# Last MLP's norm between other products, a second PSUM bank, and a later preparation, in a four-layer network

## Chip, cores and metric

The kernel runs on one core of a Trainium2 chip. The metric is the time of one execution on the device in microseconds (us); lower is better.

## What is computed

The network takes x of shape (8, 384, 32, 32), all in float32, through four layers. Two are Mamba-like (a layer norm, a projection, a short causal convolution, a selective scan over 1024 tokens with 16 states per channel, an output projection); the second of them has a gate from an attention pool, and an MLP after it. Two are depthwise convolutions with 13x13 support, the last with a pointwise product in front and a GELU behind. The change touches the MLP at the end of the second layer and the preparation of the convolutions' tables:

```python
        xs = xs + mo
        h = _ln(xs, n3_g, n3_b)
        h = jax.nn.gelu(h @ fc1_w.T + fc1_b) @ fc2_w.T + fc2_b
        xs = xs + h
...
    def bn_eval(y, gamma, beta, mean, var):
        inv = gamma * lax.rsqrt(var + BN_EPS)
        return y * inv[None, :, None, None] + (beta - mean * inv)[None, :, None, None]
```

## The kernel before

**Tiling.** An image has 1024 tokens, handled as two halves of 512. Channels lie on partitions: 384 channels are 3 tiles of 128 (KC), the inner 768 are 6 (KD), the MLP's 1536 are 12 (KF). The two Mamba layers are done as 32 units, each one image half of one layer; a unit is 48 slots of the scan. The scan itself keeps VectorE (the recurrence, L553 and L556, and the products with C, L561), ScalarE (the decays, L525) and GpSimd (the inflows, L532) busy.

**The order.** All else is placed by hand: `put(slot, f, ...)` puts a piece of work into a slot (with `first=True` ahead of the others of that slot), and the loop at L911 emits the pieces slot by slot; after the last scan step `plan.rest()` (L929) emits what is left. Within one engine, and within SP's queue, the instructions run in exactly that order, so a waiting instruction holds everything behind it on its engine. The slots stand in the table `AT` (L220) relative to a unit or an MLP. The unit's own loops end at slot 1536; slots after that are the tail.

**An MLP half.** `Mlp(b, half)` (L688) is image b, half 0 or 1; I write (7,0) and (7,1) for the last two. Its norm (`norm`, L726, slots `mlp_norm`) loads `mx` (L367), takes the mean with a product (L372), subtracts it on VectorE (L375), squares on ScalarE (L379), sums by product (L385), takes ln and exp on ScalarE (L390 to L394), and does a Newton step and the scaling on GpSimd (L400 to L409). Then come 12 "up" products of three matmuls (`mlp_up`, L695, each with a weight slice `wi` of 192 KB, five buffers), each copied out of PSUM by ScalarE (`mlp_raw`, L699), GELU in four batches of three (`table`, L456, with a table load ahead and another, L305, behind), and 3 "down" products of 12 matmuls (`mlp_down`, L708, each with two weight halves `wo` of 384 KB, three buffers). VectorE adds bias and residual (`mlp_out`, L714; the residual `mo` has one buffer) into `rows_out`, one buffer, which SP stores into `x3` (`mlp_store`, L721). Up and down products share one PSUM bank (`ps_f`, tag f); means, variances and the units' products use the two banks of `mm()` (L300).

**Around them.** The last unit's output projection (`out_product`, L604, `out_gate`, `out_add`, `out_store`, slots `out`) writes the half of `x2` that MLP (7,1) reads. `prepare` (L111) is a generator of 26 pieces, one slot each from `AT["prepare"]`: four small norms on ScalarE and VectorE, two bias vectors written to memory and read back over GpSimd's queue, six tables (load over GpSimd's queue, VectorE, store over GpSimd's queue), and at last `spread` (L148): two products and two ScalarE copies. The first unit's step sizes times u (`step_u`, L495) follow on GpSimd.

**After them.** `Depthwise` (L932) and `Pointwise` (L1006) lie in SBUF and PSUM partly where the layers' tiles were. A tile that reuses a place waits for the last use of the tile there. GpSimd fills their borders (L952) and loads the first ten groups of weights `wt` (L959, four DMAs of 128 KB each) and the images `xp` (L973).

Of the kernel before, what the change touches and what calls it, by code (L numbers as in the profile page):

```python
# [9 lines left out]
F32 = mybir.dt.float32  # L10
AF = mybir.ActivationFunctionType
ALU = mybir.AluOpType
# [4 lines left out]
P = 128  # L17
B = 8
C = 384
# [6 lines left out]
T = 512  # L26
NU = B * L // T
# [39 lines left out]
class Plan:  # L67
# [6 lines left out]
    def put(self, slot, f, *args, first=False):  # L74
        self.slots.setdefault(slot, ([], []))[0 if first else 1].append(lambda: f(*args))
# [141 lines left out]

AT = {'in_ahead': 3, 'out_ahead': 2, 'taps_ahead': 4, 'norm': (-5, -2, -1, 0, 1, 2, 3, 3, 4, 6, 8, 8, 12, 13, 14), 'x': (14, 16, 18, 24, 26, 29), 'shift': 1, 'conv': 4, 'u': 5, 'silu': ((28, 3, 0), (34, 6, 1), (40, 6, 3), (57, 6, 6)), 'hid': 2, 'ranks': (33, 34, 35), 'z': (31, 34, 36, 38, 40, 41), 'B': (40, 42, 47, 48), 'C': (42, 45, 48, 52), 'repeat': (9, 12, 12, 13), 'out': (0, 5, 9), 'out_half': 3, 'out_add': 4, 'out_gate': 2, 'res_ahead': 1, 'heads': 15, 'softmax': (16, 17, 18), 'attend': (19, 22, 25, 26), 'context': 27, 'hidden': (29, 30, 32, 35, 36, 39), 'gates': (47, 41, 46), 'mlp': 22, 'mlp_norm': (-7, 0, 1, 2, 3, 4, 5, 5, 5, 6, 6, 10, 10, 12, 12), 'mlp_plan': ((3, 62, 12, (21, 31, 42, 69), -2), (2, 42, 6, (24, 30, 42, 46), -2), (2, 40, 4, (24, 26, 34, 40), -2), (2, 42, 3, (24, 26, 34, 36), -2), (2, 42, 6, (24, 24, 36, 36), -2)), 'fold0': (-145, -128), 'shifted': 1, 'bc_out': 36, 'store': 2, 'px_ahead': 2, 'pool': (0, 4), 'norm0': (-97, -89, -86, -85, -83, -80, -77, -75, -74, -73, -72, -71, -69, -69, -68), 'soft': ((37, 2), (45, 4), (62, 6)), 'du': 1, 'du_pace': 0, 'flat_u': 1, 'inject': 0, 'y': 25, 'fold': 0, 'var': 1, 'down_gap': 0, 'first': {'x': (2, 4, 7, 10, 13, 16), 'silu': ((14, 3, 0), (22, 6, 0), (34, 6, 2), (44, 6, 6)), 'ranks': (23, 24, 26), 'z': (29, 29, 31, 33, 34, 35), 'soft': ((29, 2), (33, 4), (60, 6)), 'bc_out': 27, 'B': (32, 34, 36, 39), 'repeat': (0, 0, 1, 3), 'C': (38, 44, 44, 47)}, 'fold0_step': (1, 8), 'norm1': (-2, 0, 2, 2, 3, 4, 5, 5, 9, 9, 11, 11, 13, 14, 14), 'prepare': (-67, 4),  # L220
}


def layers(tc, k, a, vec, x0, x1, x2, x3, lasting, got):
# [8 lines left out]
    nc = tc.nc  # L233
# [7 lines left out]
    with ExitStack() as st:  # L241
# [5 lines left out]
        ps_f = st.enter_context(tc.tile_pool(name="m_f", bufs=1, space=PSUM))  # L247
# [8 lines left out]
        t = tile("fh")  # L256
# [25 lines left out]
        rows_out = wp.tile([P, T // HW, WIDE], F32, name="rows_out")  # L282
# [81 lines left out]

        def load(s, src, tag):
            s.xt = work.tile([P, KC, T], F32, tag=tag, name=tag, bufs=1)
            nc.sync.dma_start(s.xt, src.rearrange("(c p) t -> p c t", p=P)[:, :, s.cols])  # L367

        def mean(s):
            s.mean = mm()  # L370
# [25 lines left out]
        def rs_newton(s, step):  # L396

            if step == 0:
                s.rt = work.tile([P, T], F32, tag="sq", name="sq", bufs=1)
                nc.gpsimd.tensor_tensor(s.rt, s.ry, s.ry, ALU.mult)  # L400
            elif step == 1:
                nc.gpsimd.tensor_tensor(s.rt, s.rt, s.rv, ALU.mult)
            elif step == 2:
                nc.gpsimd.tensor_scalar(s.rt, s.rt, -0.5, 1.5, ALU.mult, ALU.add)
            else:
                nc.gpsimd.tensor_tensor(s.ry, s.ry, s.rt, ALU.mult)

        def scale(s, c):
            nc.gpsimd.tensor_tensor(s.xt[:, c], s.xt[:, c], s.ry, ALU.mult)  # L409


        def product(s, m):
# [274 lines left out]
        class Mlp:  # L687
            def __init__(self, b, half):  # L688
                self.b, self.half, self.cols = b, half, slice(half * T, (half + 1) * T)
                self.w, self.ps, self.hs = {}, {}, [None] * KF  # L690

        def mlp_up(s, m, c):
            if c == 0:
                s.ps[m] = ps_f.tile([P, T], F32, tag="f", name="f")
            nc.tensor.matmul(s.ps[m], s.w["in", m][:, c], s.xt[:, c], start=c == 0, stop=c == KC - 1)  # L695

        def mlp_raw(s, m):
# [6 lines left out]

        def mlp_down(s, m, f):
            if f == 0:
                s.down = ps_f.tile([P, T], F32, tag="f", name="f")
            nc.tensor.matmul(  # L708
                s.down, s.w["out", 2 * m + f // KD][:, f % KD], s.hs[f], start=f == 0, stop=f == KF - 1
            )  # L710
# [7 lines left out]

        def mlp_store(s, m):
            n = T // HW  # L720
            nc.sync.dma_start(x3[m * P : (m + 1) * P, s.half * n : (s.half + 1) * n, s.b, :], rows_out)  # L721
# [44 lines left out]
        for b in range(1, B):  # L766
            order += [(1, b - 1), (0, b + 1)] if b < B - 1 else [(1, b - 1), (1, b)]
        units = [Unit(both[n], b, half) for n, b in order for half in range(L // T)]
        done = {(s.layer.gated, s.b, s.half): i for i, s in enumerate(units)}
        assert len(units) == 2 * NU  # L770

        for i, s in enumerate(units):

            lay, at = s.layer, (i - 1) * SLOTS
            first = AT if i else {**AT, **AT["first"]}
            norm(s, lay.src[s.b], "xt", at, AT["norm"] if i > 1 else AT[f"norm{i}"])
            for d in range(KD):
                e = at + first["x"][d]
# [44 lines left out]
            for d in range(KD):  # L823
                at = i * SLOTS + (d - 2) * PER
# [48 lines left out]
        for b in range(B):  # L873
            for half in range(L // T):
                s = Mlp(b, half)
                at = max(at, (done[True, b, half] + 1) * SLOTS + AT["mlp"])
                if (at - AT["mlp"]) % SLOTS > 20:
                    at += (AT["mlp"] - at) % SLOTS
                pace_up, down, pace_down, tables, gap = AT["mlp_plan"][max(b - B + 4, 0) + (b == B - 1) * half]
                norm(s, x2[b], "mx", at, AT["mlp_norm"])  # L880
                for m in range(KF):
                    e = at + 12 + pace_up * m
                    use_in(e, s, m, fc1_w[m])
                    for c in range(KC):
                        put(e + c * pace_up // KC, mlp_up, s, m, c)
                    put(e + 2 * pace_up // KC + 1, mlp_raw, s, m, first=True)
                for j, e in enumerate(tables):
                    put(at + e, table, lambda s=s, j=j: s.hs[3 * j : 3 * j + 3], AF.Gelu_apprx_tanh)
                for m in range(KC):
                    e = at + down + (pace_down + AT["down_gap"]) * m  # L890
                    put(e, mlp_residual, s, m)
                    for f in range(KF):
                        if f % KD == 0:
                            use_out(e + f * pace_down // KF, s, 2 * m + f // KD, a["fc2"][2 * m + f // KD])
                        put(e + f * pace_down // KF, mlp_down, s, m, f)
                    put(e + pace_down, mlp_out, s, m, first=True)
                    put(e + pace_down + AT["store"], mlp_store, s, m, first=True)
                at += down + KC * (pace_down + AT["down_gap"]) + gap
# [316 lines left out]
```

## Time and profile before

| | |
|---|---|
| median of 3 runs | 6908.87 us (6908.8 to 6910.72) |
| the profiled execution's own time | 6907.97 us |
| its span, first to last instruction | 6906.2 us |
| mean granted TensorE clock | 0.923 |
| busy, PE / VectorE / ScalarE / GpSimd | 85% / 83% / 65% / 77% of the span |
| from 6200 to 6380 us: PE / VectorE / ScalarE / GpSimd busy | 144.76 / 9.07 / 52.43 / 48.80 us |
| from 6382 to 6555 us: PE busy, DMA share | 168.65 of 173 us, 1.04 |

The span falls into a start (to about 150 us), the scan loop (to about 6200), the tail of products (to 6380) and the convolutions (to the end). A line of a timeline gives start, duration, engine, line, operation, output <- inputs, shape, number of instructions, and in brackets the idle time ahead of it and what ended that. A line of the chain of waits gives start, duration, engine and line. "SPq" and "POOLq" are DMA issues on those engines' queues. Averages over the whole span say little about a single stretch: what counts is which wait ends last in it.

### The profile page before, as it was taken

The page shows a single profiled execution, that of the slowest core. Times are in us where ns is not written, and L with a number is a line of the kernel's source. Part 1 is how long each engine was busy: PE and PEld are TensorE (multiplying, and loading weights), DVE is VectorE, ACT ScalarE, POOL GpSimd, SP SyncE. Part 2 cuts the span into 40 slices and gives each one's busy share as a digit, 9 for nine tenths or more (in the row PEclk, how much of TensorE's full clock was granted, in tenths as well). Part 3 has the DMA queues.
Part 4 walks back from the last instruction along what each step waited for, and adds up shares of the span by engine and source line. Part 5 has one row for each costly group of instructions (what it writes and reads, how often), then busy time and mean ns, then how long its engine had stood idle before and what let it go on. Part 6 is the DMA issues. An engine that isn't in the chain of part 4 may idle for free. (4 is left out here: it accounts for less than half of the span.)

```text
span 6906.2 us, 76841 instructions
## 1 busy us (share of the span) xinstructions
PE 5876.6 (85%) x22562; PEld 2090.7 (30%) x22562; DVE 5750.3 (83%) x4591; ACT 4477.5 (65%) x7478; POOL 5295.9 (77%) x2864
## 2 busy tenths in 40 slices
PE   6877788888888888888888888889898888977988
PEld 2222222222322232222222232223232222323645
DVE  3899988999889888888888889888888898780837
ACT  4776666867676766767676767777677567652222
POOL 3888888888888878888888888887878888672412
PEclk7888888999999999999999999999999889989999
DMA  4665555666666666666666666666665665754979
GB/s 131 166 174 154 155 156 151 166 174 167 174 163 171 161 173 160 164 162 172 166 165 167 169 175 160 164 168 169 159 172 163 160 173 155 170 116 119 287 214 234
DMA packets 944770, 1160.04 MB, mean 168 GB/s; under 512 B 301264, under 2 KB 537344, under 8 KB 944352
## 3 DMA queue, kind: packets, MB, share of 16 engines
q1 hardware_dynamic: 788672, 1060.83, 58.7%
q10 hardware_dynamic: 140736, 50.09, 3.0%
q0 software_dynamic: 14944, 44.20, 2.3%
q8 instruction: 183, 3.00, 0.2%
q14 instruction: 235, 1.93, 0.1%
HBM read 904.67 MB, written 199.49 MB: 160 GB/s over the span
## 5 line engine op out<-in xcount | busy, mean ns | idle before, releaser
L532 POOL TENSOR_TENSOR dbu<-B,ru 128x1024 f32<-128x1024 f32 x1536 | 3585.9, 2360 | 163.0 <-DMA B<-bc 88.9
L525 ACT ACTIVATE h<-rd,A 128x512 f32<-128x512 f32 x3072 | 2117.2, 690 | 882.0 <-DVE hc L561 532.1
L553 DVE TENSOR_TENSOR_SCAN h<-h,state,dbu 128x512 f32<-128x512 f32 x1152 | 1482.6, 1287 | 208.2 <-ACT h L525 75.6
L561 DVE TENSOR_TENSOR hc<-h,C 128x1024 f32<-128x1024 f32 x1152 | 1411.1, 1225 | 146.1 <-DMA C<-bc 21.7
L556 DVE TENSOR_TENSOR_SCAN h<-h,dbu 128x1024 f32<-128x1024 f32 x576 | 1317.8, 2288 | 223.2 <-ACT h L525 156.7
L572 POOL TENSOR_TENSOR hc<-dbu,C 128x1024 f32<-128x1024 f32 x384 | 904.0, 2354 | 722.6 <-DVE dbu L556 388.0
L583 PE MATMUL acc<-hc,fold 128*32 128x512 f32 x6144 | 1151.2, 663 | 327.3 <-DVE hc L561 248.8
L415 PE MATMUL mm<-xt,wi 128*128 128x512 f32 x2232 | 1126.8, 643 | 58.4 <-ACT delta L491 19.4
L695 PE MATMUL f<-mx,wi 128*128 128x512 f32 x1152 | 606.5, 634 | 145.8 <-ACT fh L699 113.4
L415 PEld LDWEIGHTS mm<-xt,wi 128*128 128x128 f32 x2232 | 423.0, 202 | 763.4 <-issue 444.0
L604 PE MATMUL mm<-u,wo 128*128 128x512 f32 x1152 | 597.7, 660 | 65.6 <-DMA wo<-in_l_out_dram 65.4
L708 PE MATMUL f<-fh,wo 128*128 128x512 f32 x1152 | 582.6, 624 | 71.0 <-DMA wo<-in_fc_dram 60.1
L583 PEld LDWEIGHTS acc<-hc,fold 128*32 128x32 f32 x6144 | 162.5, 112 | 1131.1 <-DVE hc L561 517.4
L553 DVE TENSOR_TENSOR_SCAN dbu<-h,state,dbu 128x512 f32<-128x512 f32 x384 | 470.5, 1267 | 14.7 <-ACT h L525 8.4
L556 DVE TENSOR_TENSOR_SCAN dbu<-h,dbu 128x1024 f32<-128x1024 f32 x192 | 438.1, 2282 | 51.4 <-ACT h L525 50.6
L439 PE MATMUL mm<-xp,taps 128*64 128x512 f32 x1536 | 412.6, 658 | 21.1 <-ACT xp L425 8.1
L973 POOL DMA_DIRECT2D xp<-x x192 | 123.5, 644 | 386.7 <-PE ps L997 196.7
L997 PE MATMUL ps<-xp,wt 128*32 128x256 f32 x6144 | 345.7, 384 | 34.8 <-ACT o L1002 21.3
L305 ACT ACT_TABLE_LOAD x289 | 370.8, 1283 | 5.8 <-PEq L1203 0.7
L604 PEld LDWEIGHTS mm<-u,wo 128*128 128x128 f32 x1152 | 233.1, 211 | 435.6 <-issue 366.8
L695 PEld LDWEIGHTS f<-mx,wi 128*128 128x128 f32 x1152 | 209.9, 196 | 502.1 <-issue 252.8
L425 ACT ACTIVATE xp<-mm,b_in 64x512 f32<-64x512 f32 x384 | 261.8, 682 | 153.1 <-PE mm L415 150.6
(156 smaller groups left out, 5732.2 us busy)
## 6 DMA issues: line engine op xcount, KB each, us to landing
ru<-uu SPq DMA_DIRECT2D x1536, 128.0 KB
rd<-dd SPq DMA_DIRECT2D x1536, 128.0 KB
wi<-w_in SPq DMA_DIRECT2D x372, 192.0 KB
xp<-xp SPq DMA_DIRECT2D x384, 128.5 KB
dd<-delta SPq DMA_DIRECT2D x192, 256.0 KB
uu<-delta SPq DMA_DIRECT2D x192, 256.0 KB
wo<-in_l_out_dram SPq DMA_DIRECT2D x96, 384.0 KB
wi<-fc_w SPq DMA_DIRECT2D x192, 192.0 KB
```

Of the source, the lines that this page charges most:

```text
L415: nc.tensor.matmul(s.ps[m], w[:, c], s.xt[:, c], start=c == 0, stop=c == KC - 1)
L439: nc.tensor.matmul(s.ps[d][64 * h : 64 * h + 64], taps[:, h, j], xp[h][:, 2 * j : 2 * j + T], start=j == 0, stop=j == 1,)
L525: nc.scalar.activation(y[:, q], s.dr[d][1][h][:, q], AF.Exp, scale=s.layer.A[:, at : at + 1])
L532: nc.gpsimd.tensor_tensor(dbu, s.B[g].unsqueeze(1).to_broadcast([P, 2, T]), s.ur[d][1][h], ALU.mult)
L553: nc.vector.tensor_tensor_scan(to[:, q], y[:, q], dbu[:, q], first, ALU.mult, ALU.add)
L556: nc.vector.tensor_tensor_scan(flat_to, flat_y, flat_b, first, ALU.mult, ALU.add)
L561: nc.vector.tensor_tensor(hc, to, s.C[g].unsqueeze(1).to_broadcast([P, 2, T]), ALU.mult)
L572: nc.gpsimd.tensor_tensor(hc, y, s.C[g].unsqueeze(1).to_broadcast([P, 2, T]), ALU.mult)
L583: nc.tensor.matmul(s.acc[d][32 * r : 32 * r + 32], k["fold"], tiles[r // 2][:, r % 2], start=False, stop=n == PER - 2)
L604: nc.tensor.matmul(s.ps[m], w[:, d], s.us[d], start=d == 0, stop=d == KD - 1)
L695: nc.tensor.matmul(s.ps[m], s.w["in", m][:, c], s.xt[:, c], start=c == 0, stop=c == KC - 1)
L708: nc.tensor.matmul(s.down, s.w["out", 2 * m + f // KD][:, f % KD], s.hs[f], start=f == 0, stop=f == KF - 1)
```

## The change

The last MLP half, (7,1), becomes "alone". Its norm gets its own slots (`alone`), which place the mean, the squares and the variances between the down products of (7,0); its Newton step and scaling go to VectorE (`side`), its load of `mx` to GpSimd's queue (`queue`) and its three stores to ScalarE's queue (`store_queue`). Its odd up and down products take a bank of `mm()` in place of the one of `ps_f`. The last unit's output projection gets closer slots (`last`). `prepare` starts at slot -50, not -67. The lists in `first` are tuples before and lists after, with the same numbers. All other units and MLPs keep GpSimd and SP.

```diff
@@ -217,7 +217,7 @@
 
 
 
-AT = {... 'prepare': (-67, 4),
+AT = {... 'alone': (-12, -4, -3, -3, -2, -1, 1, 1, 1, 1, 1, 1, 1, 1, 1), 'last': {'out': (0, 2, 4), 'res_ahead': 1, 'out_gate': 1, 'out_half': 1, 'out_add': 2, 'store': 1}, 'prepare': (-50, 4),
 }
 
 
@@ -364,7 +364,7 @@
 
         def load(s, src, tag):
             s.xt = work.tile([P, KC, T], F32, tag=tag, name=tag, bufs=1)
-            nc.sync.dma_start(s.xt, src.rearrange("(c p) t -> p c t", p=P)[:, :, s.cols])
+            s.queue.dma_start(s.xt, src.rearrange("(c p) t -> p c t", p=P)[:, :, s.cols])
 
         def mean(s):
             s.mean = mm()
@@ -397,16 +397,16 @@
 
             if step == 0:
                 s.rt = work.tile([P, T], F32, tag="sq", name="sq", bufs=1)
-                nc.gpsimd.tensor_tensor(s.rt, s.ry, s.ry, ALU.mult)
+                s.side.tensor_tensor(s.rt, s.ry, s.ry, ALU.mult)
             elif step == 1:
-                nc.gpsimd.tensor_tensor(s.rt, s.rt, s.rv, ALU.mult)
+                s.side.tensor_tensor(s.rt, s.rt, s.rv, ALU.mult)
             elif step == 2:
-                nc.gpsimd.tensor_scalar(s.rt, s.rt, -0.5, 1.5, ALU.mult, ALU.add)
+                s.side.tensor_scalar(s.rt, s.rt, -0.5, 1.5, ALU.mult, ALU.add)
             else:
-                nc.gpsimd.tensor_tensor(s.ry, s.ry, s.rt, ALU.mult)
+                s.side.tensor_tensor(s.ry, s.ry, s.rt, ALU.mult)
 
         def scale(s, c):
-            nc.gpsimd.tensor_tensor(s.xt[:, c], s.xt[:, c], s.ry, ALU.mult)
+            s.side.tensor_tensor(s.xt[:, c], s.xt[:, c], s.ry, ALU.mult)
 
 
         def product(s, m):
@@ -689,9 +689,17 @@
                 self.b, self.half, self.cols = b, half, slice(half * T, (half + 1) * T)
                 self.w, self.ps, self.hs = {}, {}, [None] * KF
 
+                self.alone = b == B - 1 and half == 1
+                self.side = nc.vector if self.alone else nc.gpsimd
+                self.queue = nc.gpsimd if self.alone else nc.sync
+                self.store_queue = nc.scalar if self.alone else nc.sync
+
+            def bank(self, m):
+                return mm() if self.alone and m % 2 else ps_f.tile([P, T], F32, tag="f", name="f")
+
         def mlp_up(s, m, c):
             if c == 0:
-                s.ps[m] = ps_f.tile([P, T], F32, tag="f", name="f")
+                s.ps[m] = s.bank(m)
             nc.tensor.matmul(s.ps[m], s.w["in", m][:, c], s.xt[:, c], start=c == 0, stop=c == KC - 1)
 
         def mlp_raw(s, m):
@@ -704,7 +712,7 @@
 
         def mlp_down(s, m, f):
             if f == 0:
-                s.down = ps_f.tile([P, T], F32, tag="f", name="f")
+                s.down = s.bank(m)
             nc.tensor.matmul(
                 s.down, s.w["out", 2 * m + f // KD][:, f % KD], s.hs[f], start=f == 0, stop=f == KF - 1
             )
@@ -718,7 +726,7 @@
 
         def mlp_store(s, m):
             n = T // HW
-            nc.sync.dma_start(x3[m * P : (m + 1) * P, s.half * n : (s.half + 1) * n, s.b, :], rows_out)
+            s.store_queue.dma_start(x3[m * P : (m + 1) * P, s.half * n : (s.half + 1) * n, s.b, :], rows_out)
 
 
         put = plan.put
@@ -766,6 +774,8 @@
         for b in range(1, B):
             order += [(1, b - 1), (0, b + 1)] if b < B - 1 else [(1, b - 1), (1, b)]
         units = [Unit(both[n], b, half) for n, b in order for half in range(L // T)]
+        for s in units:
+            s.side, s.queue = nc.gpsimd, nc.sync
         done = {(s.layer.gated, s.b, s.half): i for i, s in enumerate(units)}
         assert len(units) == 2 * NU
 
@@ -829,16 +839,17 @@
                 put(at + AT["y"], y_out, s, d, first=True)
 
             at = (i + 1) * SLOTS
+            out = {**AT, **AT["last"]} if i == 2 * NU - 1 else AT
             for m in range(KC):
-                e = at + AT["out"][m]
-                put(e - AT["res_ahead"], residual, s, m)
+                e = at + out["out"][m]
+                put(e - out["res_ahead"], residual, s, m)
                 if lay.gated:
-                    put(e + AT["out_gate"], out_gate, s, m)
+                    put(e + out["out_gate"], out_gate, s, m)
                 use_out(e, s, m, lay.w["out"][m])
                 for j in range(2):
-                    put(e + AT["out_half"] * j, out_product, s, m, j)
-                put(e + AT["out_add"], out_add, s, m, first=True)
-                put(e + AT["out_add"] + AT["store"], out_store, s, m, first=True)
+                    put(e + out["out_half"] * j, out_product, s, m, j)
+                put(e + out["out_add"], out_add, s, m, first=True)
+                put(e + out["out_add"] + out["store"], out_store, s, m, first=True)
             if not lay.gated:
                 continue
 
@@ -877,7 +888,7 @@
                 if (at - AT["mlp"]) % SLOTS > 20:
                     at += (AT["mlp"] - at) % SLOTS
                 pace_up, down, pace_down, tables, gap = AT["mlp_plan"][max(b - B + 4, 0) + (b == B - 1) * half]
-                norm(s, x2[b], "mx", at, AT["mlp_norm"])
+                norm(s, x2[b], "mx", at, AT["alone" if s.alone else "mlp_norm"])
                 for m in range(KF):
                     e = at + 12 + pace_up * m
                     use_in(e, s, m, fc1_w[m])
```

More of the change, by code (lines that the diff above doesn't have):

```diff
@@ L216, in prepare @@
     yield
-AT = {'in_ahead': 3, 'out_ahead': 2, 'taps_ahead': 4, 'norm': (-5, -2, -1, 0, 1, 2, 3, 3, 4, 6, 8, 8, 12, 13, 14), 'x': (14, 16, 18, 24, 26, 29), 'shift': 1, 'conv': 4, 'u': 5, 'silu': ((28, 3, 0), (34, 6, 1), (40, 6, 3), (57, 6, 6)), 'hid': 2, 'ranks': (33, 34, 35), 'z': (31, 34, 36, 38, 40, 41), 'B': (40, 42, 47, 48), 'C': (42, 45, 48, 52), 'repeat': (9, 12, 12, 13), 'out': (0, 5, 9), 'out_half': 3, 'out_add': 4, 'out_gate': 2, 'res_ahead': 1, 'heads': 15, 'softmax': (16, 17, 18), 'attend': (19, 22, 25, 26), 'context': 27, 'hidden': (29, 30, 32, 35, 36, 39), 'gates': (47, 41, 46), 'mlp': 22, 'mlp_norm': (-7, 0, 1, 2, 3, 4, 5, 5, 5, 6, 6, 10, 10, 12, 12), 'mlp_plan': ((3, 62, 12, (21, 31, 42, 69), -2), (2, 42, 6, (24, 30, 42, 46), -2), (2, 40, 4, (24, 26, 34, 40), -2), (2, 42, 3, (24, 26, 34, 36), -2), (2, 42, 6, (24, 24, 36, 36), -2)), 'fold0': (-145, -128), 'shifted': 1, 'bc_out': 36, 'store': 2, 'px_ahead': 2, 'pool': (0, 4), 'norm0': (-97, -89, -86, -85, -83, -80, -77, -75, -74, -73, -72, -71, -69, -69, -68), 'soft': ((37, 2), (45, 4), (62, 6)), 'du': 1, 'du_pace': 0, 'flat_u': 1, 'inject': 0, 'y': 25, 'fold': 0, 'var': 1, 'down_gap': 0, 'first': {'x': (2, 4, 7, 10, 13, 16), 'silu': ((14, 3, 0), (22, 6, 0), (34, 6, 2), (44, 6, 6)), 'ranks': (23, 24, 26), 'z': (29, 29, 31, 33, 34, 35), 'soft': ((29, 2), (33, 4), (60, 6)), 'bc_out': 27, 'B': (32, 34, 36, 39), 'repeat': (0, 0, 1, 3), 'C': (38, 44, 44, 47)}, 'fold0_step': (1, 8), 'norm1': (-2, 0, 2, 2, 3, 4, 5, 5, 9, 9, 11, 11, 13, 14, 14), 'prepare': (-67, 4),
@@ new lines @@
+AT = {'in_ahead': 3, 'out_ahead': 2, 'taps_ahead': 4, 'norm': (-5, -2, -1, 0, 1, 2, 3, 3, 4, 6, 8, 8, 12, 13, 14), 'x': (14, 16, 18, 24, 26, 29), 'shift': 1, 'conv': 4, 'u': 5, 'silu': ((28, 3, 0), (34, 6, 1), (40, 6, 3), (57, 6, 6)), 'hid': 2, 'ranks': (33, 34, 35), 'z': (31, 34, 36, 38, 40, 41), 'B': (40, 42, 47, 48), 'C': (42, 45, 48, 52), 'repeat': (9, 12, 12, 13), 'out': (0, 5, 9), 'out_half': 3, 'out_add': 4, 'out_gate': 2, 'res_ahead': 1, 'heads': 15, 'softmax': (16, 17, 18), 'attend': (19, 22, 25, 26), 'context': 27, 'hidden': (29, 30, 32, 35, 36, 39), 'gates': (47, 41, 46), 'mlp': 22, 'mlp_norm': (-7, 0, 1, 2, 3, 4, 5, 5, 5, 6, 6, 10, 10, 12, 12), 'mlp_plan': ((3, 62, 12, (21, 31, 42, 69), -2), (2, 42, 6, (24, 30, 42, 46), -2), (2, 40, 4, (24, 26, 34, 40), -2), (2, 42, 3, (24, 26, 34, 36), -2), (2, 42, 6, (24, 24, 36, 36), -2)), 'fold0': (-145, -128), 'shifted': 1, 'bc_out': 36, 'store': 2, 'px_ahead': 2, 'pool': (0, 4), 'norm0': (-97, -89, -86, -85, -83, -80, -77, -75, -74, -73, -72, -71, -69, -69, -68), 'soft': ((37, 2), (45, 4), (62, 6)), 'du': 1, 'du_pace': 0, 'flat_u': 1, 'inject': 0, 'y': 25, 'fold': 0, 'var': 1, 'down_gap': 0, 'first': {'x': [2, 4, 7, 10, 13, 16], 'silu': [[14, 3, 0], [22, 6, 0], [34, 6, 2], [44, 6, 6]], 'ranks': [23, 24, 26], 'z': [29, 29, 31, 33, 34, 35], 'soft': [[29, 2], [33, 4], [60, 6]], 'bc_out': 27, 'B': [32, 34, 36, 39], 'repeat': [0, 0, 1, 3], 'C': [38, 44, 44, 47]}, 'fold0_step': (1, 8), 'norm1': (-2, 0, 2, 2, 3, 4, 5, 5, 9, 9, 11, 11, 13, 14, 14), 'alone': (-12, -4, -3, -3, -2, -1, 1, 1, 1, 1, 1, 1, 1, 1, 1), 'last': {'out': (0, 2, 4), 'res_ahead': 1, 'out_gate': 1, 'out_half': 1, 'out_add': 2, 'store': 1}, 'prepare': (-50, 4),
```

## Prediction

> **What bounds the kernel now.** I read the page's slices first: VectorE and GpSimd are busy through the selective-scan loop, the last scan ends near 6200 us, and then two things follow that the change touches: a tail of MLP products (6200 to 6380) and two depthwise convolutions (6382 to the end, PE busy in 168.65 of the first one's 173 us). The chain of waits, in order of time, shows what sets the tail:
>
> ```profile
> 6265.25 7.13 PE f L708 x16
> 6272.39 2.58 PE mm L372 x6
> 6274.96 3.43 PE f L708 x8
> ...
> 6286.02 1.27 POOL sq L402
> 6288.07 1.26 POOL rs_y L406
> 6289.43 1.26 POOL mx L409
> 6290.73 5.50 PE f L695 x6
> 6296.26 0.70 ACT fh L699
> 6297.00 2.86 PE f L695 x6
> ```
>
> TensorE's order is the chain. Its "down" products (L708) of MLP (7,0) end at 6278.4, then the norm of MLP (7,1) runs alone on ScalarE and GpSimd until 6290.7, then each "up" product (L695) waits for ScalarE to empty the one bank. TensorE's timeline gives the pace and the two larger holes:
>
> ```profile
> 6311.48 2.84 PE L695 MATMUL f<-mx,wi 128*128 128x512 f32 x6 [0.78 <-ACT fh L699]
> 6324.34 4.31 PE L695 MATMUL f<-mx,wi 128*128 128x512 f32 x6 [6.41 <-ACT fh L699]
> 6343.91 10.57 PE L708 MATMUL f<-fh,wo 128*128 128x512 f32 x24 [0.78 <-ACT fh L699]
> 6355.32 10.57 PE L708 MATMUL f<-fh,wo 128*128 128x512 f32 x24 [0.84 <-DVE rows_out L714]
> 6373.93 5.42 PE L708 MATMUL f<-fh,wo 128*128 128x512 f32 x12 [1.78 <-DMA wo<-in_fc_dram]
> 6381.87 18.50 PE L997 MATMUL ps<-xp,wt 128*32 128x256 f32 x305 [2.52 <-issue]
> ```
>
> Six records are one product of three matmuls. The queues around the norm, SP's and then the DMA windows:
>
> ```profile
> 6265.60 13.98 SPq L721 DMA_DIRECT2D x<-rows_out  x2
> 6279.63 38.66 SPq L310 DMA_DIRECT2D wi<-fc_w  x12
> ```
>
> ```profile
> 6280.00:6283.00 3.00, 2.22 (x4) 0.56 (x4) 0.00 (x0) 0.63 (x1) 0.00 (x0) 1.00 0.87 154
> 6283.00:6287.00 4.00, 0.00 (x0) 0.00 (x0) 0.00 (x0) 1.78 (x3) 2.02 (x2) 0.92 0.75 208
> 6287.00:6290.00 3.00, 0.00 (x0) 0.00 (x0) 0.00 (x0) 0.00 (x0) 2.75 (x4) 0.50 0.00 0
> ```
>
> The reader should see that the first weight slice of the last MLP is issued only at 6279.63, behind the last store of MLP (7,0), and that its traffic fits into the norm's 12 us. The last three figures are clock, DMA share and GB/s.
>
> For the moved preparation, the start of the kernel (PE, ACT, POOL, PE timelines):
>
> ```profile
> 60.47 0.71 PE L150 MATMUL mm<-fh 4*128 4x96 f32 x2 [11.67 <-DMA fh<-b_flat]
> ...
> 61.22 0.24 ACT L151 COPY b<-mm 128x96 f32<-128x96 f32 x1 [13.51 <-PE mm L150]
> ...
> 101.65 0.54 POOL L212 DMA_DIRECT2D k_rows<-hc  x1 [5.37 <-DVE hc L210]
> 102.21 1.28 POOL L495 TENSOR_TENSOR delta<-delta,u 128x512 f32<-128x512 f32 x1
> ...
> 146.07 4.37 PE L372 MATMUL mm<-xt,avg 128*128 128x512 f32 x6 [25.43 <-DMA xt<-in_x_dram]
> ```
>
> **What the Trainium skill says.** "DMA: Bandwidth & Descriptors", section "Queues, rings and completion order": each DMA engine goes round the rings that have work, a packet of several descriptors at a time. The trace agrees that rings slow each other: by its completions a lone 192 KB slice took 2.24 us (issued 6296.25, done 6298.49), and 4.0 to 5.1 us (6303.5 to 6307.5, 6307.1 to 6312.2) beside GpSimd's convolution weights. "TensorE: Matmul & The Clock Gate", section "What's actually happening": an idle window of about 3.4 us halves the clock until a busy one has passed. Here the clock is 0.50 after the norm and the product at 6290.73 took 5.50 instead of 2.86 us. "ScalarE: Activation LUTs", "What ACT_TABLE_LOAD costs": 1283 ns; L456 and L305 show 1.28.
>
> **The change part by part.** Its own span is 6906.2, with 1.77 us around it 6907.97; the median of the runs is 0.90 higher.
>
> *Preparation, 17 slots later.* On GpSimd and VectorE nothing else stands in slots -67 to -25, so their order doesn't change; ScalarE's four small norms move, but to before its first shift_in as now. The only step that changes places is the last, `spread`: two products and copies, which now stand ahead of the third input product and hold PE for 11.67 and ACT for 13.51 us. PE and ACT then run about 13.8 us earlier (48.8 instead of 62.58). I cost it at nothing: GpSimd reaches the step sizes (L495) only after the preparation's last store, 102.2, though their input is there at 98.2 already; SP's flat stores, repeats and loads follow from that, and TensorE, ScalarE and VectorE all wait for SP's load of the next `xt` until 146.07. Bounds: 9.6 us gained (the first scan at 127.70 could start when its operands are there, near 118), 10 us lost (eight DMA round trips in series, each up to 1.2 us longer, as 5.15 against 3.97 us is in this stretch now).
>
> *Last output projection, closer slots.* The same 18 matmuls lie before the last five "up" products of (7,0) instead of among them: fewer slots to hide bank waits in, but x2's last store leaves at 6226 instead of 6239. From 6200.72 I add 4.47 (half clock), 36 x 0.857, bank waits of 1.05 at the products left alone, and ScalarE's table step (4.25) ahead of the last copy: the downs start at 6242.6, against 6242.46. Nothing gained.
>
> *The norm beside the downs.* `mx` is loaded from GpSimd's queue when the last up has read it (6240.6); 768 KB at the 250 to 350 GB/s seen there lands by about 6247, wanted at 6257.5. Behind it on GpSimd stand only the convolution's memsets and weights. Mean and variances go between downs, 3 x 0.86 more than now, one bank wait (0.85) hidden under a variance, so the downs end at 6280.3 instead of 6278.4. Seven VectorE operations (half of L561's 1.225, so 0.65 each) end near 6280.0: covered. **What is late next** is the weight slice: SP still has the store of (7,0) ahead of it, which waits for the last down and its 0.75 us addition. It is issued at 6281.5; now it completes 5.7 us after its issue (6285.35 in the trace). But GpSimd's early weights, free to start at 6250, stop at the fourth tile: by the tile sizes in order of first use, `wt3` and `wt4` lie on `sq`, `rs_y` and `rs_v`, so 28 of 40 loads begin at 6280, on top of that store and slice. I take 8.5 us (bounds 5.7 and 20): the first up at 6290.0. Gain 0.7.
>
> *Two banks.* First up to first down is 53.2 us now. With two banks: 12 x 2.57 (the pace of L604 without waits), 2.8 for the cold clock, and at the double table step ScalarE is busy 0.70 + 8.54 + 0.70 while PE has two banks to fill, so 5.2 us idle instead of 6.4 plus a product, and 1.7 for the clock after it: 40.5. Gain 12.7.
>
> *Downs and stores.* The bank waits of 0.84 go, but `mo` has one buffer, and on SP the next weights wait behind its load: the fourth lands some 0.9 late, the sixth about as late relative to its addition as now. 34.7 instead of 35.44: gain 0.7, bounds -1 and 2. The stores on ScalarE's queue hold only the convolution's copies, which come later anyway. The convolutions move forward whole (TensorE-bound).
>
> Sum 0.7 + 12.7 + 0.7 = 14.1: 6907.97 - 14.1 = 6893.9 in the profiled execution, 6894.8 for the median.
>
> **The rivals.** (1) The forecast, 0.70; its own range 6890 to 6899 (slice 6 to 13 us, downs as bounded). (2) Preparation was on the path: for it, VectorE idles 26.35 us on ScalarE at the start; against it, the `xt` load at the end of SP's queue. 14.1 + 9.6: 6885. 0.10. (3) The slice starves: the store's 2048 small pieces and the slice get through only when 28 weight loads (0.58 to 0.72 us each, 18 us) are issued: first up at 6302, 11 lost, 6906.5. For it, SP's order; against it, slices beside those loads took only 2 to 3 us more. 0.13. (4) Slower: the preparation's round trips beside six shifts and tap loads grow so far that GpSimd reaches L495 at 120 instead of 102: 14.1 - 18, 6912.8. It decides above 1.8 us for each of the eight; now it is 1.2 at worst. 0.04. The rest, 0.03, is an order I misread, a late `mx` say.
>
> **How the numbers follow.** 0.2%, about what a measurement can tell from no change, is 13.8 us, so the forecast lies on the edge of it. Faster: somewhat over half of (1), 0.38, and (2): 0.48. Slower 0.05, with part of (4) and of what I misread. Same: 0.47. Range 6885 to 6906, from (2) to (3).
>
> **What would show it.** Right: L400 to L409 of the last MLP on VectorE inside the downs, no GpSimd wait before the first L695, but one for `wi`; L695 at 2.57 with one hole of about 5 us; GpSimd's `wt` loads in two batches; L495 still near 102 and the first scan stage unmoved behind `xt`. Wrong: L495 off 102 by more than 2, the first L695 after 6295 or before 6287, or convolutions that take other than their 524 us.

## The result, and the profile after

Fourteen runs of each kernel on one chip: the kernel before has a median of 6899.98 us (6892.24 to 6918.12), the changed one 6886.91 us (6870.9 to 6893.76). The ratio of the means is 0.9974 with a 95% interval from 0.9966 to 0.9983, that is 12 to 23 us faster. The three runs of 6908.8 to 6910.72 us that the prediction was made from lie in the upper part of the fourteen.

The profiled execution of the changed kernel has a span of 6870.5 us, at the lower end of its runs and 35.7 us below the profiled one of before (6906.2). Line numbers from L364 to L689 stay, those of the MLP and what follows are 8 to 11 higher. I call *tail* what lies between the first matmul of the last output projection (6200.72 before, 6182.40 after) and the end of the last down; *arrival* is that first matmul.

First TensorE's timeline of the changed kernel, in the tail:

```profile
6254.83 5.31 PE L716 MATMUL f<-fh,wo 128*128 128x512 f32 x12
6271.30 5.11 PE L703 MATMUL f<-mx,wi 128*128 128x512 f32 x6 [11.16 <-DMA wi<-fc_w]
6276.25 2.74 PE L703 MATMUL mm<-mx,wi 128*128 128x512 f32 x6
...
6299.31 4.54 PE L703 MATMUL f<-mx,wi 128*128 128x512 f32 x6 [4.88 <-ACT fh L707]
...
6328.48 5.42 PE L716 MATMUL mm<-fh,wo 128*128 128x512 f32 x12 [1.45 <-DMA wo<-in_fc_dram]
...
6341.38 5.42 PE L716 MATMUL f<-fh,wo 128*128 128x512 f32 x12 [2.33 <-DMA wo<-in_fc_dram]
6349.32 1.05 PE L1008 MATMUL ps<-xp,wt 128*32 128x256 f32 x13 [2.52 <-issue]
```

The products now alternate between a bank of `f` and one of `mm`, 2.57 us apart, where each had waited 0.78 us for ScalarE's copy. The hole at the double table step is 4.88 us, where it was 6.41. Between the two MLPs TensorE no longer waits for the norm: it waits 11.16 us for the first weight slice. SP's queue shows why, and GpSimd's timeline what else began just then:

```profile
6249.06 12.26 SPq L729 DMA_DIRECT2D x<-rows_out  x2
6261.37 30.84 SPq L310 DMA_DIRECT2D wi<-fc_w  x12
```

```profile
6260.27 5.17 POOL L970 DMA_DIRECT2D wt<-k_rows  x9 [23.28 <-PE f L716]
```

The second store of the first line waits for the last down and its addition, and the slice stands behind it. The chain of waits of the changed kernel runs through the same place:

```profile
6260.18 0.76 DVE rows_out L722
...
6260.96 0.37 SPq L729
...
6261.37 9.79 DMA wi<-fc_w
...
6271.30 5.11 PE f L703 x6
```

At the start of the changed kernel (GpSimd's timeline, then TensorE's):

```profile
103.99 0.54 POOL L212 DMA_DIRECT2D k_rows<-hc  x1 [5.12 <-DVE hc L210]
104.55 1.27 POOL L495 TENSOR_TENSOR delta<-delta,u 128x512 f32<-128x512 f32 x1
```

```profile
81.53 0.46 PE L150 MATMUL mm<-fh 4*128 4x96 f32 x2
...
149.14 1.20 PE L372 MATMUL mm<-xt,avg 128*128 128x512 f32 x1 [28.64 <-DMA xt<-in_x_dram]
```

The stall of 11.67 us ahead of `spread` is gone, and nothing was gained by it: the first step sizes (L495) start 2.3 us later than before, and the second unit's mean, which waits for SP's `xt` load, 3.1 us later.

By stages, in these two executions: start 3.1 us lost, scan loop 21.4 us gained (from the second centring, L375 at 150.48 and 153.62, to the arrival), tail 14.2 us gained (178.63 to 164.40), convolutions 3.1 us gained (526.84 to 523.72 from the last down's end). The diff has no edit in the loop or in the convolutions. So more than half of what this pair shows lies where nothing was changed, and that is what the experiments had to clear up first.

### The profile page after: what moved, and what is told of

The parts are those of the page before. It is cut to its first block, busy times and chain, and to the rows that moved or that the text cites. A ratio compares the mean times of both kernels' runs of the same rounds, so it can differ in the third digit from the quotient of the medians.

```text
span 6870.5 us, 76836 instructions
## 1 busy us (share of the span) xinstructions
PE 5851.1 (85%) x22562; PEld 2082.8 (30%) x22562; DVE 5755.9 (84%) x4598; ACT 4475.3 (65%) x7478; POOL 5285.7 (77%) x2858
## 5 line engine op out<-in xcount | busy, mean ns | idle before, releaser
L415 PE MATMUL mm<-xt,wi 128*128 128x512 f32 x2232 | 1116.9, 638 | 57.2 <-ACT delta L491 18.9
L703 PE MATMUL f<-mx,wi 128*128 128x512 f32 x1116 | 589.0, 635 | 141.7 <-ACT fh L707 99.9
L415 PEld LDWEIGHTS mm<-xt,wi 128*128 128x128 f32 x2232 | 419.9, 201 | 754.5 <-issue 435.5
L1008 PE MATMUL ps<-xp,wt 128*32 128x256 f32 x6144 | 343.8, 381 | 34.7 <-ACT o L1013 21.1
L580 PE MATMUL acc<-u,skip 128*128 128x512 f32 x384 | 226.1, 673 | 153.2 <-DVE u L588 150.6
```

Of the source, the lines that this page charges most:

```text
L415: nc.tensor.matmul(s.ps[m], w[:, c], s.xt[:, c], start=c == 0, stop=c == KC - 1)
```

## The experiments

The runs came in three sets, each on one chip with its own runs of the kernel before (medians 6917.26, 6918.08 and 6908.61 us). Ratios are to those; e5 and e8 were timed five times and e9 six, and runs without an interval once. Times in the profiles: first up, tail and arrival as above; "ups" from the first up to the first matmul of the downs, "downs" from there to the end, "conv" from the end of the downs.

| run | ratio, interval | arrival | first up | ups | downs | tail | conv |
|---|---|---|---|---|---|---|---|
| before, first profile | | 6200.7 | 90.0 | 53.2 | 35.4 | 178.6 | 526.8 |
| r_before | | 6207.4 | 90.2 | 54.4 | 35.9 | 180.4 | 534.5 |
| after, first profile | 0.9974, 0.9966 to 0.9983 | 6182.4 | 88.9 | 40.1 | 35.4 | 164.4 | 523.7 |
| r_after | 0.9981, 0.9973 to 0.9989 | 6196.2 | 89.7 | 39.3 | 36.0 | 164.9 | 531.7 |
| e1_prep_back | 0.9982, 0.9973 to 0.9991 | 6191.5 | 90.9 | 40.7 | 35.3 | 167.0 | 530.3 |
| e2_prep_alone | 0.9998, 0.9989 to 1.0006 | 6200.2 | 90.6 | 54.3 | 35.4 | 180.3 | 531.1 |
| e3_banks_alone | 0.9987, 0.998 to 0.9995 | 6196.2 | 88.4 | 40.7 | 33.1 | 162.2 | 529.1 |
| e4_one_bank | 0.9998, 0.999 to 1.0005 | 6198.3 | 89.6 | 53.0 | 35.5 | 178.1 | 534.2 |
| e5_slice_free | 0.9963, 0.9949 to 0.9977 | 6195.3 | 79.8 | 38.5 | 35.6 | 153.8 | 532.5 |
| e7_gelu_apart | | 6198.8 | 90.4 | 35.3 | 35.2 | 160.9 | 532.6 |
| e8_best | 0.9957, 0.9945 to 0.9969 | 6198.2 | 85.3 | 34.3 | 31.2 | 150.9 | 533.7 |
| e9_order_kept | 0.9943, 0.9928 to 0.9958 | 6201.9 | 81.4 | 32.7 | 31.2 | 145.2 | 532.3 |
| e11_prep_later | | 6199.8 | 88.7 | 39.8 | 35.3 | 163.8 | 531.1 |

### The parts, one at a time

**Only the preparation undone (e1_prep_back), and only the preparation made (e2_prep_alone).**

```diff
-AT = {... 'prepare': (-50, 4),      # e1, in the changed kernel
+AT = {... 'prepare': (-67, 4),
-AT = {... 'prepare': (-67, 4),      # e2, in the kernel before
+AT = {... 'prepare': (-50, 4),
```

> The changed kernel with the preparation at its old slots and all else kept. Theory A (the pieces are independent; the moved preparation delays the start; the long scan loop varies from execution to execution by itself): GpSimd's first step-size product (L495) back from 104.55 to about 102.2, the second centring from 153.62 to about 150.5, so 3.1 us gained against the changed kernel; the tail from the first product of the last output projection to the last down stays at 164.4, the convolutions at 523.7. Total 6884 by the medians, against 6887 for the changed kernel; the loop anywhere in 6025 to 6052. Theory B (the moved preparation itself speeds up the scan loop, by the order in which loads are issued behind it): the loop comes back to 6050, and the total to about 6900.

> The kernel before with only the preparation moved by 17 slots. Theory A: L495 near 104.5, second centring near 153.6, tail 178.6 and convolutions 526.8 as in the kernel before; ratio 1.0004, that is 3 us slower than the kernel before, hardly to be told from no change. Theory B: the scan loop near 6029 instead of 6050 and the ratio near 0.9975.

L495 starts at 104.33 in e1 and at 104.80 in e2, the second centring at 154.60 and 155.04: with the preparation back in its old slots the start is as late on this chip as with it moved, and theory A's figures for e1's start (102.2 and 150.5) missed. Theory B falls: e1 keeps its gain (0.9982) and e2 has none (0.9998), and the loop of e2 (6045.2 us from the second centring) is longer, not shorter, than that of e1 (6036.9).

**Only the two banks (e3_banks_alone), and all but the two banks (e4_one_bank).**

```diff
+        def bank(s, m):                      # e3, in the kernel before
+            return mm() if s.b == B - 1 and s.half == 1 and m % 2 else ps_f.tile([P, T], F32, tag="f", name="f")
...
-                s.ps[m] = ps_f.tile([P, T], F32, tag="f", name="f")
+                s.ps[m] = bank(s, m)
...
-                return mm() if self.alone and m % 2 else ps_f.tile([P, T], F32, tag="f", name="f")   # e4, in the changed one
+                return ps_f.tile([P, T], F32, tag="f", name="f")
```

> The kernel before with only the two PSUM banks in turn for the last MLP. Theory A: first up to last product's down 40.1 to 41 us instead of 53.2, so 12.5 us of the tail; the start as before (150.5); the convolutions 526.8, since the last MLP's stores stay on SP's queue; ratio 0.9982. Theory C (most of the tail's gain needs the norm beside the downs as well, since with the norm in front ScalarE and TensorE begin cold and wait for slices): 47 us or more, ratio 0.9990 or above.

> The changed kernel with one PSUM bank for the last MLP, all else kept. Theory A: tail 164.4 + 13 = 177.4 us; convolutions 523.7, as their 3.1 us come from the stores that left SP's queue; start 153.6; about 1 us net faster than the kernel before (3.1 lost at the start, 1.2 + 3.1 gained), ratio 0.9998. Theory C: tail 171 or less, ratio 0.9990 or less.

The ups take 40.7 us in e3 and 53.0 us in e4: in the ups the banks alone are worth 12 to 14 us wherever they are put, and the rest of the change alone gives a ratio of 0.9998. Theory C falls by the ups; e3's ratio alone would not decide it. What I had not expected is that e3's tail (162.2) is the shorter one, 2 to 3 us under the whole change. TensorE's timeline of e3 between the MLPs:

```profile
6284.60 5.34 PE L698 MATMUL f<-mx,wi 128*128 128x512 f32 x6 [7.78 <-POOL mx L409]
...
6352.93 5.42 PE L711 MATMUL f<-fh,wo 128*128 128x512 f32 x12 [1.64 <-DMA wo<-in_fc_dram]
```

With the norm in front, TensorE waits 7.78 us for GpSimd, and the first up comes 88.4 us after the arrival; with the norm beside the downs it waits 11.16 us for the slice and comes after 88.9 and 89.7 us. The slice takes the norm's place to about a microsecond: over the six profiles with the norm beside the downs and the store on SP's queue the first up comes after 88.7 to 90.9 us, over the four with the norm in front after 88.4 to 90.6.

e3 also has one wait for `wo` in its downs instead of two. The order of issue differs there. First e3 (SP's queue), then the changed kernel (SP's queue, then ScalarE's), behind the first addition of the downs:

```profile
6336.99 0.37 SPq L321 DMA_DIRECT2D wo<-in_fc_dram  x1
6337.41 0.43 SPq L724 DMA_DIRECT2D x<-rows_out  x1
```

```profile
6322.70 0.33 SPq L711 DMA_DIRECT2D mo<-x  x1
6323.13 0.85 SPq L321 DMA_DIRECT2D wo<-in_fc_dram  x2
```

```profile
6322.70 25.29 ACTq L729 DMA_DIRECT2D x<-rows_out  x3
```

With the last stores on SP's queue the store leaves 0.42 us behind the weight half; on ScalarE's queue it leaves 0.43 us ahead of it. All four profiles with these stores on SP's queue have one wait for `wo` in the downs (1.64 to 2.19 us), all seven with the stores on ScalarE's queue and the residual loads on SP's have two (together 3.50 to 4.37 us with two banks, 1.58 us in e4 with one). So the move of the stores, which is part of the change, probably costs the downs with two banks about 2 us; no run makes this move alone. The 16 to 18 us that e3's profile shows in the tail are more than its ratio allows (3 to 14 us); one execution is one sample here too.

### The same kernels again

> The changed kernel again, unaltered, for a second profile on the chip of the runs sent with it. If the loop's difference between the two first profiles (21 us) is scatter between executions: its loop anywhere in 6030 to 6055, stages of 185.5 or 183.1 us falling out differently, while the tail stays at 164.4 within 2.5 us; ratio 0.9980, that is the tail's 14.1 us alone. If it belongs to the change: loop below 6036 again and ratio 0.9970 or less.

> The kernel before again, unaltered. Scatter: loop anywhere in 6030 to 6055, tail 178.6 within 2 us, convolutions 524 to 532. If the convolutions' 3.1 us and the start's 3.1 us belong to the change, then they show against the changed kernel's second profile with the same sign and size; if they are scatter, they do not.

The tail repeats: 164.9 and 180.4 us. The rest does not. The changed kernel arrives at 6196.2 instead of 6182.4, its convolutions take 531.7 us instead of 523.7, and among the other runs the convolutions take 529.1 to 534.5 us, in no order with the queue that the last stores use (529.1, 531.1 and 534.5 on SP's, 530.3 to 534.2 on ScalarE's, in both cases with the banks or without). The forecasts of 523.7 and 526.8 us for e1 to e4 all missed. In the second pair the changed kernel's convolutions are again 2.9 us shorter, the sign and nearly the size that were named ahead as speaking for the change, while its start is only 1.0 us later; but e1 to e4, on one chip, spread over 5 us without any order by the change. I take the 3.1 us for scatter, which is likely and not shown. The loop was scatter too, as far as these profiles can tell: twelve of the thirteen arrive between 6191 and 6208, whatever their preparation, and the first profile of the changed kernel is the one outlier. A few us for the change are not excluded (the four profiles of kernels with the norm in front arrive at 6201 on average, the other nine at 6196).

Where a loop differs can be seen. Six stages of it (between two centrings of `xt` or `mx`, every sixth one, from 858 us on in before) take 187.0 to 189.1 us in the first profile of before and 183.8 to 188.2 us in that of after; together that is 1128.4 against 1114.3 us, 14.1 of the 18.3 us between the two arrivals. It does not belong to the change: the shortest sums of all are those of e2 (1112.9 us) and e1 (1113.2 us), one made from each kernel. One such stage in both, from its centring to VectorE's L684, 2.8 and 2.1 us short of the next centring, by the view of windows (length, then busy time of TensorE, weight loads, VectorE, ScalarE, GpSimd; at the end clock, DMA share, GB/s), before and then after:

```profile
3876.81:4062.45 185.64, 164.93 (x527) 57.13 (x528) 165.18 (x118) 142.15 (x252) 154.69 (x76) 0.94 0.63 170
```

```profile
3868.50:4051.57 183.07, 163.74 (x528) 56.31 (x529) 165.09 (x118) 141.95 (x252) 154.66 (x76) 0.96 0.63 171
```

The work is the same; the granted clock is 0.94 against 0.96. Inside, before and then after, by TensorE's timeline:

```profile
3991.32 0.83 PE L667 MATMUL mm<-ctx,wi 128*128 128x1 f32 x6 [2.91 <-ACT u L446]
...
3999.38 4.54 PE L415 MATMUL mm<-xt,wi 128*128 128x512 f32 x6
```

```profile
3982.45 1.44 PE L667 MATMUL mm<-ctx,wi 128*128 128x1 f32 x6 [2.36 <-ACT u L446]
...
3990.21 2.84 PE L415 MATMUL mm<-xt,wi 128*128 128x512 f32 x6
```

In both the granted clock falls to half about here, as the first L667 (1.44 instead of 0.83 us, after) and L415 (4.54 instead of 2.84 us, before) show; it stays there longer in before. The two stretches at half clock, before and then after:

```profile
3992.80:4003.00 10.20, 9.28 (x23) 3.67 (x20) 9.00 (x6) 5.76 (x14) 9.02 (x5) 0.51 0.93 202
```

```profile
3982.20:3989.00 6.80, 6.28 (x22) 2.32 (x22) 6.59 (x5) 5.11 (x12) 6.80 (x4) 0.50 0.78 214
```

"TensorE: Matmul & The Clock Gate", section "What's actually happening", of the Trainium skill describes such a drop after an idle window of about 3.4 us, in windows that run freely; here waits of 2.91 and 2.36 us, both shorter, go with it, and it lasts about three and about two times 3.4 us. What made it last longer in before, the second wait (0.92 against 0.28 us) or where the windows fell, was not tried. By the trace's record of the clock it is at half over this whole stage for 23.9 us in before and 16.8 in after, and the same holds for the loop as a whole: it is longer, by and large, where more of it runs at half clock (874 us of the 6028.8 in after, 894 of 6040.2 in r_after, 942 of 6050.2 in before, 953 of 6052.3 in r_before; over all thirteen profiles the two go together with a correlation of 0.86). Which of them drives the other is not shown, since a wait can also lower the clock.

### The stall that took the norm's place

```diff
-                self.store_queue = nc.scalar if self.alone else nc.sync      # e5
+                self.store_queue = nc.scalar if b == B - 1 else nc.sync
```

> The changed kernel with the stores of the last but one MLP on ScalarE's queue too, so that no store stands on SP's queue ahead of the last MLP's first weight slice. If that queue place is what makes PE idle 11.16 us: the slice is issued when SP has issued the last mo load, some 11 us before the last down ends, and the first up follows the last down within 1 us, at full clock; the tail 164.4 - 10.3 - 2.3 = 151.8; ratio to the kernel before 0.9962. If the wait is the bandwidth that the convolution's weight loads take, or the norm's end, it stays above 5 us and the tail above 158.

```profile
6267.16 7.03 PE L716 MATMUL f<-fh,wo 128*128 128x512 f32 x16
6275.03 2.84 PE L703 MATMUL f<-mx,wi 128*128 128x512 f32 x6 [0.85 <-DVE rows_out L722]
```

In TensorE's timeline of e5 the first up follows the last down after a bank wait of 0.85 us, at full speed; it comes 9 to 10 us earlier, and the tail is 153.8 us against 151.8 expected. So the queue place of the store was the cause of the wait, not the norm's end nor the weight loads by themselves. Here the norm beside the downs does gain what it could: 162.2 (banks alone) to 153.8 us.

```diff
-AT = {... 'mlp_plan': (... (2, 42, 6, (24, 24, 36, 36), -2)), ...      # e7, in the changed kernel
+AT = {... 'mlp_plan': (... (2, 42, 6, (20, 26, 32, 36), -2)), ...
```

> The changed kernel with the last MLP's first two Gelu steps at slots 20 and 26 instead of both at 24, and the third at 32. If the hole in the last MLP's ups is the double table step: no wait above 1 us between the ups, first up to first down of the last product 39.3 - 4.88 - 2.4 = 32 us, tail 157.5. If a table step stops TensorE each time because two banks are filled sooner than ScalarE is back (4.23 + 0.69 us against 2 x 2.57): up to three holes of 2 us, and 36 us or more.

```profile
6304.85 2.74 PE L703 MATMUL mm<-mx,wi 128*128 128x512 f32 x6
6308.20 2.84 PE L703 MATMUL f<-mx,wi 128*128 128x512 f32 x6 [0.61 <-ACT fh L707]
...
6324.53 10.57 PE L716 MATMUL f<-fh,wo 128*128 128x512 f32 x24 [0.61 <-ACT fh L707]
```

The hole was the double table step: set apart, the first step and the third, ahead of the downs, stop TensorE for 0.61 us each, as these lines of e7 show, and the second not at all. The ups take 35.3 instead of 40.1 us. I had expected 32: the subtraction started from 39.3 (r_after) and took 7.3 us off for the hole, but these two waits remain, and the first product is slower than the one it was reckoned from (5.46 against 4.43 us).

**All together, and what went wrong with it (e8_best, e9_order_kept).** e8 takes e5's and e7's edits, the preparation at its old slots, and:

```diff
-            nc.sync.dma_start(s.res, x2[s.b][m * P : (m + 1) * P, s.cols])
+            (nc.scalar if s.alone else nc.sync).dma_start(s.res, x2[s.b][m * P : (m + 1) * P, s.cols])
...
-        for g in range(self.EARLY):
+        for g in (0, 1, 2, 5, 6, 7, 8, 9, 3, 4):
```

> The changed kernel with the preparation at its old slots, the stores as in e5_slice_free, the last MLP's residual loads on ScalarE's queue, its first two Gelu steps at slots 20 and 26 instead of both at 24 (the third at 32), and the two convolution weight tiles that overlie the norm's tiles loaded last. Each stall taken to be its own: 151.8 as in e5_slice_free, less the hole at the double table step (4.88 and 1.7 of cold clock), less the two waits for wo (1.45 + 2.33): tail 141.5; ratio 0.9947. If the stalls only move (the table steps then stop ScalarE twice, the wo loads wait for buffers rather than for the mo load): tail 148 or more, ratio 0.9957.

The downs (31.2 us, no wait for `wo`) came as expected and the ups (34.3 us) about 2 us over the subtraction, but the first up came at 85.3, 5.6 us later than in e5. VectorE's timeline of e8, the additions at the end of the downs:

```profile
6267.33 0.75 DVE L722 SCALAR_TENSOR_TENSOR rows_out<-f,vecs,mo 128x512 f32<-128x512 f32 x1 [9.55 <-DMA x<-rows_out]
6282.77 0.75 DVE L722 SCALAR_TENSOR_TENSOR rows_out<-f,vecs,mo 128x512 f32<-128x512 f32 x1 [2.25 <-DMA x<-rows_out]
...
6351.75 0.75 DVE L722 SCALAR_TENSOR_TENSOR rows_out<-f,vecs,mo 128x512 f32<-128x512 f32 x1 [12.17 <-DMA x<-rows_out]
```

There is one `rows_out`, and the addition waits until the previous store has read it. Loading the two blocked weight tiles last had let five more groups, 20 loads, run during the downs, beside those stores. e9 takes that one edit back:

> e8_best with the convolution's weight tiles loaded in their old order again, all else kept. If the reordered loads, now running beside the downs of the last but one MLP, are what slowed the stores of rows_out (VectorE waited 9.55, 2.25 and 12.17 us for them in e8_best): those waits fall to 7.2 us or less at the first and to none at the last, the downs of the last but one MLP end at 79 as in e5_slice_free, and the tail is 153.8 - 4.88 - 2.4 - 1.80 - 2.19 = 142.5, ratio 0.9947. If the stores are slowed by the move to ScalarE's queue or by the residual loads there, the waits stay and the tail is 148 or more.

```profile
6270.14 0.75 DVE L722 SCALAR_TENSOR_TENSOR rows_out<-f,vecs,mo 128x512 f32<-128x512 f32 x1 [7.04 <-DMA x<-rows_out]
6282.41 0.75 DVE L722 SCALAR_TENSOR_TENSOR rows_out<-f,vecs,mo 128x512 f32<-128x512 f32 x1 [0.45 <-PE f L716]
...
6349.10 0.75 DVE L722 SCALAR_TENSOR_TENSOR rows_out<-f,vecs,mo 128x512 f32<-128x512 f32 x1 [11.58 <-DMA x<-rows_out]
```

The first two waits shrink as expected (the first was 7.15 us in e5 too, on e8's chip and in the old order) and the tail is 145.2 us against 142.5 expected; the last stays (11.58 us), since the downs themselves are now short enough for the store to be late, and the convolutions start 4.56 instead of 2.52 us after the downs. A second `rows_out` should take it away; it was not tried. e9 has the lowest ratio, 0.9943 (0.9928 to 0.9958), 29 to 50 us under the kernel before and by the ratios some 20 us under the changed one; its interval overlaps those of e5 and e8.

### The preparation, once more

```diff
-AT = {... 'prepare': (-50, 4),      # e11, in the changed kernel
+AT = {... 'prepare': (-33, 4),
```

> The changed kernel with the preparation another 17 slots later. If the moved preparation delays GpSimd's first step-size product (L495, means 104.9 at the old slots and 106.3 at the new ones, four runs each on this chip): later again, above 107.4, and the second centring above 157.6. If the difference is scatter between executions: L495 within 103 to 107.4, the second centring within 152 to 157.5.

(The means named there come from two chips, not one.) GpSimd's timeline of this run:

```profile
104.28 0.54 POOL L212 DMA_DIRECT2D k_rows<-hc  x1 [3.54 <-DVE fh L186]
104.81 3.75 POOL L190 DMA_DIRECT2D fh<-in_dw_dram  x7
108.58 1.27 POOL L495 TENSOR_TENSOR delta<-delta,u 128x512 f32<-128x512 f32 x1
```

Here only two tables are stored ahead of L495 and it comes at 108.58; the second centring comes at 165.83. So the preparation's slots do reach the start. But the arrival is 6199.8, in the middle of all: the eight to fifteen microseconds by which its second centring is later than in the other profiles are not found again at the end of the loop. Over all profiles L495 starts at 102.2 to 106.0 with the old slots (six runs, mean 104.1) and at 103.5 to 107.4 with the new ones (six, mean 105.5); a delay of about 1.4 us, smaller than the spread within each, which I count as likely and not as shown.

## Why the prediction was right or wrong

**The step that failed is the base, "Its own span is 6906.2, with 1.77 us around it 6907.97; the median of the runs is 0.90 higher".** It took three runs within 2 us of each other, and one execution, as the kernel's time, and everything outside the edits as fixed. The three were high: over fourteen runs the median is 6899.98, 8.9 us lower. 6899.98 - 14.1 = 6885.9, and 6886.91 was measured; of the 7.9 us between forecast and result, 8.9 are the base and 1.0, the other way, is all the rest. (By the means the base is 6.0 us too high and the gain 17.7 us instead of 14.1, which its interval of 12 to 23 us includes.) The scatter that this step left out also makes the profiled pair differ by 35.7 us, where the tail differs by 14.2. The unchanged kernel scatters over 26 us in fourteen runs, twice the gain that was forecast. The bound of 13.8 us for what a measurement can tell was too coarse: the two measurements of the changed kernel (0.9974 and 0.9981) have intervals of about 6 us to each side, and both exclude no change.

That 6886.91 lies inside the range of 6885 to 6906 is luck. The forecast's own range, 6890 to 6899, missed it; the lower end came from the rival in which the preparation was on the path, and e2 refutes that one.

**Two banks: right.** Forecast 53.2 to 40.5 us; measured 53.2 to 40.1, and 54.4 to 39.3 in the second pair; e3 and e4 show it in both directions. The hole of 5.2 us was 4.88, and its cause, the double table step, is confirmed by e7.

**The slice behind the store: right, one size off.** First up 0.7 us earlier was forecast, 1.1 and 0.6 measured. The agreement is in part luck: the first product of (7,0)'s downs came 1.8 us earlier than forecast, so the slice was issued that much earlier, and it landed after 9.8 us, not 8.5. The weight loads come in two batches as said, and the second begins 1.1 us ahead of the slice (6260.27); before, with the same store ahead of it and no weight loads, it took 5.7 us. How the 9.8 us divide between store and loads was not tried. The rival in which it starves was wrong by its size: 9.8 us, within the bounds of 5.7 and 20. That the norm's place would bring next to nothing alone was right; e5 shows that it was this queue place, and what it hid: 9 to 10 us.

**Downs: mis-sized.** 34.7 us forecast; 35.4 and 36.0 measured, so nothing gained. The two waits for `wo` were seen coming: the fourth half was put at 0.9 us late and made TensorE wait 1.45 us (1.75 in the second profile); the sixth was to be as late relative to its addition as before, 1.78 + 0.84 us, and made it wait 2.33 and 2.62 us. That the stores on ScalarE's queue would cost the downs nothing is the part that probably failed: there the store leaves ahead of the weight half, as the comparison with e3 shows. With the residual load off SP's queue they go, and the downs take 31.2 us (e8, e9).

**Last output projection at 0: right within its scatter.** Its downs start 1.7 us earlier in the first pair (40.06 against 41.74 us after the arrival), but 40.26 against 40.06 in the second.

**Preparation at 0: the reason failed, the result stood.** L495 was to stay near 102 and the first scan stage unmoved; L495 moved 2.3 us in the first pair, which was named as a sign of error. From the first store (L140) to L495 GpSimd takes 57.7 us in that pair instead of 55.7. But the whole change of slots is worth nothing measurable: 0.9998 (0.9989 to 1.0006) alone. The rivals that put it on the path, either way, fall with it: -9.6 and +18 us both lie outside that interval (8 us faster to 4 us slower).

**Convolutions at 524 us: off by 3.1 in the pair, probably by scatter.** In the other runs they take longer than in either of the first two profiles, and these runs show no order by the change, though both pairs have the changed kernel ahead by some 3 us.

## What to carry to other kernels

Before a gain of 0.2% is forecast or believed, look at how far the unchanged kernel scatters and where: three runs that agree say little about the fourteenth, and a pair of profiles differs also in stages that nobody touched. Compare stages, not spans, and trust a stage that repeats. When an engine is freed of a wait, look at what stands in the next queue ahead of its next input: here the norm moved out of the way, and a weight slice behind an unrelated store took its place; the 9 to 10 us came only when the store went to another queue.

## What the runs showed of the hardware

One stage of one program, with the same work in it, takes 188.42 and 189.05 us from centring to centring in two executions of the kernel before, and 185.12 and 187.35 us in two of the changed one, which has the same loop; the clock is at half for 23.9, 30.7, 16.8 and 23.9 us of it. Six such stages add up to between 1112.9 and 1128.4 us over the thirteen profiles. In all thirteen traces the granted clock is 1.00 or 0.50 and nothing between, and each stretch at 0.50 lasts a whole number of times 3.41 us; the two shown above last 10.24 and 6.83 us.

And transfers that nobody waits for lengthen those that somebody does: a store of `rows_out` kept VectorE waiting 9.55 us with 20 more weight loads beside it, and 7.04 us with those loads held back (e8 and e9).
